# Audio tower on one core: sine slots of 32 parts with the cosine indices in place, x in eight single places, a plan that counts overlap, and early exponentials held together

## The chip, the cores and the metric

One core of a Trainium2 chip runs the whole program in one launch. The metric is device time in microseconds (us). The engines named below are PE (TensorE, matmuls), DVE (VectorE), ACT (ScalarE), POOL (GpSimd) and SP (SyncE, which here issues every DMA). Each engine works through its own list of instructions in a fixed order, and waits for another engine only through semaphores.

## The reference

Thirty-two sequences of 160,000 samples are cut into S = 313 frames of 512. A cosine transform gives h. One attention layer and one "lookup" feed-forward layer are added to it:

```python
h = einsum('bfh,kh->bfk', frames, D)
h = h + attn(layernorm(h))     # 8 heads of 64, rotary with scale,
                               # softmax * decay matrix, norm per head, silu gate
# feed-forward: 256 units n, 512 features d
theta = layernorm(h)[..., None, :] / (1 + abs(W)) + B
idx   = mod(round(theta * 4096 / 2pi), 4096)
out   = (cos_t[idx] * attn_cos).sum(-1) @ proj_cos.T \
      + (sin_t[idx] * attn_sin).sum(-1) @ proj_sin.T
h = h + silu(out)
```

The feed-forward part dominates. For each of 32 x 313 positions it needs one sine and one cosine for each of 256 x 512 pairs of unit and feature: 32,768 "parts" of 313 positions on 128 partitions (32 sequences x 256 units x 4 feature chunks), each with two transcendental values per element.

## The kernel before

**Parts, slots and rounds.** A part is one unit n, one chunk c of 128 features and one sequence: 128 x 313 elements. The 256 units are cut into 8 blocks of 32 (`UNITS`); a sequence passes through all 8, one a round, and sequences join in a staggered way given by `STARTS`. In round rd the "ring" holds the r sequences that are under way; there are 42 rounds, and r climbs from 1 to 8, stays there for 22 rounds, and falls to 1 again. Within a round, parts are taken chunk by chunk, unit by unit and sequence by sequence, and packed into *slots* of `SLOT` = 24 parts (16 at r = 1).

**What a slot does** (function `ffn_round`):

- DVE computes the table index as int16 from x and the unit's factor and offset, one instruction for each run of neighbouring sequences of one unit (line 800, `index`). A run that a slot's end cuts becomes two instructions. DVE then adds a quarter turn into a second int16 tile (`quarter`, line 816) and reduces both tiles to 12 bits with one AND/XOR (`mask`, line 823). So a slot takes two of the `N_IX` = 5 index tiles.
- ACT takes the sine of the one tile and then of the other (`sines`, line 837): two instructions of 24 x 313 = 7512 elements a slot, each into two of the `N_TRIG` = 5 half-slot f32 tiles.
- PE sums over features with 32-column weights "hot" (line 860), accumulating over the round in PSUM; at the round's end the sums are copied (line 882) and stored in DRAM.

**x.** A chunk of all the ring's sequences is loaded from DRAM by one DMA into one of `N_X` = 2 buffers of 8 places (line 785), so the next chunk's load stands in the other buffer.

**Attention.** Sequence 0 has a hand-written opening (`opening`). Each further sequence goes through `attention`, spread over the rounds by due times. It uses one set of buffers and four PSUM banks. For each pair of heads the scores' row maximum is taken and subtracted (lines 448 and 452, both DVE, into `prob`), and later `exps` takes the exponential of all eight heads in two plan operations of four heads each: one ACT instruction each (line 469) with sums by DVE (line 484), or, where the ring is narrow, twelve small ones each with the sum accumulated (line 473). The second of the two has key -1e9, so it goes first among what is ready on ACT; after it a tiny Silu activation (line 477) brings the table that holds Silu and Sin back.

**What sets the order.** The order on every engine is written out ahead of the run by a list scheduler, class `Plan`. Each operation has a key (its due place), an engine, a duration in ns, and what it reads and writes. `emit` simulates the engines: on each it takes, among what is ready by its own clock, the operation with the smallest key. An operation that waits for one on another engine becomes ready `WAIT` or `SLACK` ns after it, one that waits for its own engine at once. `lend` hands a DVE operation that has an ACT form (index, copies) to ACT when the plan sees ACT with nothing to do: line 806 is the index on ACT. SP's DMAs are planned likewise, and SP's queue runs them strictly in that order.

Of the kernel before, what the change touches and what calls it, by code (L numbers as in the profile page):

```python
# [36 lines left out]
SLOT = 24  # L37
HALF = SLOT // 2

STARTS = (0, 2, 4, *range(6, 35))  # L40
AFF = -985.0
SLACK, PATIENT, QUICK = 800.0, 18000, (2, 32)
FROM, TO, LEAD, NARROW = -900.0, -899.0, 8.0, 2
# [12 lines left out]
class Plan:  # L56
# [5 lines left out]
    OWN = 0.8  # L62

    def __init__(self):
        self.ops = []
        self.other = {}
        self.wait = []
        self.slack = self.WAIT

    def add(self, key, eng, dur, fn, r=(), w=(), other=None):  # L70
        if other:
            self.other[len(self.ops)] = other
        self.wait.append(self.slack)
        self.ops.append((key, eng, dur, fn, tuple(r), tuple(w)))
# [5 lines left out]
    def lend(self, t, e, at, free, ready, coming):  # L80

        if ready["ACT"] or free["ACT"] > t or (coming["ACT"] and coming["ACT"][0][0] <= t):
            return None
        while coming["DVE"] and coming["DVE"][0][0] <= t:
            _, i = heapq.heappop(coming["DVE"])
            heapq.heappush(ready["DVE"], (self.ops[i][0], i))
        held = sorted(ready["DVE"])[int(free["DVE"] <= t):]
        for o in sorted((o for o in held if o[1] in self.other),
                        key=lambda o: (self.other[o[1]][0] > self.ops[o[1]][2], o)):
            if True:  # L90
                start = max(free["ACT"], at[o[1]])
                if coming["ACT"] and coming["ACT"][0][0] < start + self.OWN * self.other[o[1]][0]:
                    continue
                ready["DVE"].remove(o)
                heapq.heapify(ready["DVE"])
                return o[1], start
        return None

    def emit(self):
# [31 lines left out]
        left = len(ops)  # L131
        while left:
            best = None
            for e in free:
                if ready[e]:
# [5 lines left out]
                if best is None or t < best[0]:  # L141
                    best = (t, e)
            t, e = best
            lent = self.lend(t, e, at, free, ready, coming)
            if lent:
                i, t = lent
                e = "ACT"
                dur, fn = self.other[i]
            else:
# [5 lines left out]
            fn()  # L155
            free[e] = t + dur
            end = t + dur + (self.LAND if e == "SP" else 0.0)
            left -= 1
            for j in after[i]:
                same = ops[j][1] == e and e != "SP"  # L160
                at[j] = max(at[j], end + (0.0 if same else self.wait[i]))
# [3 lines left out]
        return max(free.values())  # L165
# [3 lines left out]
def tile_audio_tower(ctx: ExitStack, tc: tile.TileContext, t: dict, out: bass.AP):  # L169
# [6 lines left out]
    N_X, N_IX, N_TRIG, N_HOT, N_PA = 2, 5, 5, 4, 4  # L176
# [185 lines left out]
    def attention(plan, keys, sq, x, eng, swap_m=None, early=False, quick=False):  # L362
# [13 lines left out]
        def residual(key, load):  # L376
            for i in range(NT):
# [20 lines left out]
        rows(plan, step("rows"), x, x.xnT, wv_d, (x.k("xnT"),), range(NT - 1, -1, -1),  # L398
             ("wv_d",))
        copy(plan, step("copy"), eng, NT * HOP, x.v[:N], W3.rearrange("n j (g d) -> n j g d", d=P),  # L400
             x.banks(0, 1, 2), hs)
        plan.add(step(), "POOL", 4000, lambda: nc.gpsimd.memset(x.v[0:1, : NT - 1], 0.0), (), hs)  # L402
# [4 lines left out]
        def rotary(g):  # L407
            key = step("rotary")
            y = x.sets[g % len(x.sets)]
            qk, kq = x.qk[g % 2], x.k("u", g % 2)  # L410
# [6 lines left out]
            else:  # L417
                copy(plan, key, eng, 2 * S, x.raw, y.W[:, 0:2, :S], y.banks(0, 1), probs[-1:])
                for i in range(2):
# [10 lines left out]
                     probs[-2:], (kq,))  # L430
# [27 lines left out]
        for half in range(2):  # L458
            for g in (2 * half, 2 * half + 1):
                rotary(g)  # L460
            for g in (2 * half, 2 * half + 1):
                scores(g)


        key = step("exps")
        for a0 in (0, H // 2):
            def exps(a0=a0):
                if eng == "DVE":
                    nc.scalar.activation(x.prob[:N, a0 : a0 + H // 2], x.prob[:N, a0 : a0 + H // 2],  # L469
                                         AF.Exp)  # L470
                for a in range(a0, a0 + H // 2):
                    for i in range(NT if eng == "ACT" else 0):
                        nc.scalar.activation(x.prob[:N, a, i, :], x.prob[:N, a, i, :], AF.Exp,
                                             accum_out=x.sm[:N, i, a : a + 1])
                if a0:

                    nc.scalar.activation(x.lu[:1, 0:1], x.lu[:1, 0:1], AF.Silu)  # L477
            plan.add(-1e9 if a0 else key, "ACT", 1400 + (7700 if eng == "ACT" else 3350), exps,
                     probs[a0 : a0 + H // 2] if early else probs if not a0 else (),
                     [*probs[a0 : a0 + H // 2], x.k("sm", a0), x.k("lu")])  # L480
        if eng == "DVE":
# [264 lines left out]
    def ffn_round(plan, k0, blk, ring, final):  # L746
# [8 lines left out]
        full = SLOT if r > 1 else 4 * N_HOT  # L755
        sizes = [full, 8, 4, 4] if not k0 else [4, 4, 8, *[full] * 7] if final else [full]
        slots, room = [[]], sizes[-1]
        for c in range(NC4):
            for n in range(UNITS):
                b0 = 0  # L760
                while b0 < r:
                    if not room:
                        slots.append([])
                        sizes = sizes[: max(1, len(sizes) - 1)]
                        room = sizes[-1]
                    nb = min(room, r - b0)
                    slots[-1].append((n, c, b0, nb, sizes[-1] - room))
                    b0 += nb
                    room -= nb
        banks, hot, xs, fs = {}, {}, {}, {}  # L770
        key = k0
        for parts in slots:
            first, last = parts is slots[0], parts is slots[-1]
            L = sum(o[3] for o in parts)
            E = L * S
            for c in dict.fromkeys(o[1] for o in parts):
                if c not in xs:
                    y, fz = xs[c], fs[c] = place("xT", N_X), place("f", N_X)
                    plan.add(key - 10, "SP", DMA_NS,
                             lambda c=c, fz=fz: nc.sync.dma_start(  # L780
                                 new("f", fz, [P, 2, UNITS], bufs=N_X), f_d[blk, :, :, c, :]),
                             ("f_d",), (("f", fz),))
                    if k0 or c > 1:
                        plan.add(key - 10, "SP", DMA_NS,
                                 lambda c=c, y=y: nc.sync.dma_start(
                                     xT[:, y, : r * S], xT_d[:, c, sq0 * S : (sq0 + r) * S]),
                                 [("xT_d", sq) for sq in ring], (("xT", y),))
            for n, c in dict.fromkeys((o[0] // 4 * 4, o[1]) for o in parts):
                if (n, c) not in hot:
                    z = hot[n, c] = place("hot", N_HOT)  # L790
                    plan.add(key - 4, "SP", DMA_NS,
# [4 lines left out]
            x = [place("ix", N_IX) for _ in range(2)]  # L796
            for n, c, b0, nb, at in parts:
                def index(x=x, n=n, b0=b0, nb=nb, at=at, y=xs[c], fz=fs[c]):
# [3 lines left out]
                        xT[:, y, b0 * S : (b0 + nb) * S],  # L802
                        f[:, 0, n : n + 1], f[:, 1, n : n + 1], ALU.mult, ALU.add)
                def index_act(x=x, n=n, b0=b0, nb=nb, at=at, y=xs[c], fz=fs[c]):
# [3 lines left out]
                        xT[:, y, b0 * S : (b0 + nb) * S], AF.Identity,  # L808
                        bias=f[:, 1, n : n + 1], scale=f[:, 0, n : n + 1])
                plan.add(key, "DVE", 276 + 0.521 * nb * S, index,  # L810
                         (("f", fs[c]), ("xT", xs[c])), (("ix", x[0], at),),
# [6 lines left out]
            plan.add(key, "DVE", 170 + 0.26 * E, quarter, every(x[0]), every(x[1]))  # L818

            def mask(x=x, E=E):  # L820

                for i in ([slice(x[0], x[1] + 1)] if x[0] < x[1] else [slice(i, i + 1) for i in x]):
                    nc.vector.tensor_scalar(ix[:, i, :E], ix[:, i, :E], LUT - 1, LUT // 2,  # L823
                                            ALU.bitwise_and, ALU.bitwise_xor)
            plan.add(key, "DVE", 170 + 0.26 * 2 * E, mask, (), [*every(x[0]), *every(x[1])])
            for k in (1, 0):
# [11 lines left out]
                plan.add(key, "ACT", 115 + 0.8333 * E, sines, every(x[1 - k]),  # L838
# [6 lines left out]

                for h, z in enumerate(w):
# [24 lines left out]
                if not last:  # L871
                    continue
                for bk, p in enumerate(banks[k]):
# [14 lines left out]
                    def store(k=k, q=q, sq=sq):  # L888
# [6 lines left out]
                        for g in range(4):  # L895
# [5 lines left out]
                             [("sums_d", sq + b, blk) for b in range(q)])  # L901

# [57 lines left out]
    xT = pools["work"].tile([P, N_X, RING * S], F32, name="xT")  # L960

    def opening(plan):

        spaces = [[trig.rearrange("p i e -> p (i e)"), 0, 4 * HALF * S],
                  [trig[:, 4], NC4 * S, HALF * S],
                  [ix.rearrange("p i e -> p (i e)").bitcast(F32), 0, N_IX * SLOT * S // 2],
                  [xT[:, 1], S, RING * S],
                  [xT[:, 0], S, RING * S]]
# [57 lines left out]
        spare = trig[:, 4, : NC4 * S].rearrange("p (c s) -> p c s", s=S)  # L1026
        xts = [xT[:, 0, :S], xT[:, 1, :S], spare[:, 2], spare[:, 3]]
        k_xts = [("xT", 0), ("xT", 1), ("trig", 4), ("trig", 4)]
# [251 lines left out]
        stands = [*(("pa", z) for z in range(N_PA)), *(("trig", z) for z in range(N_TRIG) if z != 4),  # L1280
# [25 lines left out]
    for rd in range(n_rounds):  # L1306
        events.append((key_of[rd], 3, lambda rd=rd: ffn_round(
        plan, key_of[rd], rd % life, rings[rd], rd == n_rounds - 1)))
# [15 lines left out]
    for i in range(len(times) - 1):  # L1324
        k, e = times[i] + shift[i], times[i + 1]
        narrow = len(rings[int(np.searchsorted(key_of, k, "right")) - 1]) <= NARROW
        events.append((k, 1, lambda k=k, e=e, i=i, narrow=narrow: attention(
            plan, lambda x: k + (e - k) * x, 2 + i, A, "ACT" if narrow else "DVE",
            quick=QUICK[0] <= i + 2 < QUICK[1])))
    for _, _, go in sorted(events, key=lambda y: y[:2]):  # L1330
        go()
    with tc.manual_schedule():
# [123 lines left out]
```

## Time and profile before

| what | value |
|---|---|
| time, median of 3 runs | 18152.65 us (18149.81 to 18154.47) |
| time of the profiled execution | 18155.45 us |
| its span, first to last instruction | 18153.7 us |
| instructions | 322,090 |
| mean granted TensorE clock | 0.935 |
| DMA | 943.16 MB, mean 52 GB/s |
| sines: ACT line 837 | 2780 instructions |
| index on DVE, line 800 / on ACT, line 806 | 5329 / 206 instructions |
| wait of SP's queue for PE before "hot" loads, line 792 | 7425.7 us in 1216 waits |

The span is 1.75 us shorter than that execution's time. A busy time is the union of an engine's instructions; two neighbours on ACT or DVE can overlap, so the sum of durations is larger than the busy time. What an engine did not fill of the span is idle time, and how that lies over the stages is read from the busy times in windows.

### The profile page before, as it was taken

The page shows a single profiled execution, that of the slowest core. Times are in us where ns is not written, and L with a number is a line of the kernel's source. Part 1 is how long each engine was busy: PE and PEld are TensorE (multiplying, and loading weights), DVE is VectorE, ACT ScalarE, POOL GpSimd, SP SyncE. Part 2 cuts the span into 40 slices and gives each one's busy share as a digit, 9 for nine tenths or more (in the row PEclk, how much of TensorE's full clock was granted, in tenths as well). Part 3 has the DMA queues.
Part 4 walks back from the last instruction along what each step waited for, and adds up shares of the span by engine and source line. Part 5 has one row for each costly group of instructions (what it writes and reads, how often), then busy time and mean ns, then how long its engine had stood idle before and what let it go on. Part 6 is the DMA issues. An engine that isn't in the chain of part 4 may idle for free.

```text
span 18153.7 us, 322090 instructions
## 1 busy us (share of the span) xinstructions
PE 14314.5 (79%) x146495; PEld 6447.3 (36%) x146495; DVE 17132.7 (94%) x12295; ACT 17989.7 (99%) x3448; POOL 126.5 (1%) x40
## 2 busy tenths in 40 slices
PE   8888888887778777878777787777777777766667
PEld 4434433433333333333333333333333333322222
DVE  8999999999999999999999999999999999888888
ACT  7999999999999999999999999999999999999999
POOL 0000000000000000000000000000000000000000
PEclk9999999999999999999999999999999999989889
DMA  3222211111111111111111111111111111100011
GB/s 115 74 63 64 67 56 57 53 51 47 45 52 53 53 52 41 53 54 51 51 50 47 53 53 53 52 41 53 54 51 50 48 48 54 46 28 27 28 33 58
DMA packets 603597, 943.16 MB, mean 52 GB/s; under 512 B 121290, under 2 KB 344138, under 8 KB 589430
## 3 DMA queue, kind: packets, MB, share of 16 engines
q1 hardware_dynamic: 602230, 922.56, 16.4%
q8 instruction: 1148, 18.81, 0.4%
q14 instruction: 219, 1.79, 0.0%
HBM read 818.35 MB, written 103.94 MB: 51 GB/s over the span
## 4 chain that ended last, share of the span: by engine, by line
ACT 40%; PE 18%; DVE 8%; issue 7%; DMA 0%; ACTq 0%; SPq 0%; DVEq 0%
ACT trig L837 40%; PE PS L860 15%; DVE ix L800 3%; DVE ix L823 2%; PE PS L341 2%; DVE ix L816 1%; PE PS L357 1%; ACT a_prob L469 0%; DMA a_u<-in_frames 0%; DVE part L882 0%; PE PS L561 0%; ACT L477 0%; DVE a_h L267 0%; PE PS L523 0%; ACTq L837 0%
## 5 line engine op out<-in xcount | busy, mean ns | idle before, releaser
L837 ACT ACTIVATE trig<-ix 128x7512 f32<-128x7512 int16 (+2 forms) x2780 | 17384.1, 6346 | 50.1 <-PE PS L860 30.6
L860 PE MATMUL PS<-trig,hot 128*32 128x313 f32 x131072 | 10449.9, 463 | 3662.4 <-ACT trig L837 3594.1
L860 PEld LDWEIGHTS PS<-trig,hot 128*32 128x32 f32 x131072 | 4391.7, 117 | 9590.2 <-ACT trig L837 4876.7
L800 DVE TENSOR_SCALAR ix<-xT,f 128x2504 int16<-128x2504 f32 (+7 forms) x5329 | 6418.7, 1264 | 90.4 <-ACT trig L837 67.1
L823 DVE TENSOR_SCALAR ix<-ix 128x7512 int16<-128x7512 int16 (+3 forms) x1668 | 5583.9, 3362 | 42.5
L816 DVE TENSOR_SCALAR ix<-ix 128x7512 int16<-128x7512 int16 (+2 forms) x1390 | 2908.8, 2093 | 553.3 <-ACT trig L837 450.7
L357 PE MATMUL PS<-a_xnT,a_ring 128*128 128x313 f32 x4960 | 1468.1, 439 | 8.9 <-DVE a_prob L425 6.9
L341 PE MATMUL PS<-a_ring,a_u 128*105 128x512 f32 x2232 | 1067.4, 611 | 53.6 <-DMA a_u<-in_frames 19.6
L357 PEld LDWEIGHTS PS<-a_xnT,a_ring 128*128 128x128 f32 x4960 | 893.4, 189 | 588.4 <-issue 276.5
L341 PEld LDWEIGHTS PS<-a_ring,a_u 128*105 128x105 f32 x2232 | 349.9, 171 | 629.3 <-issue 585.3
L341 PE MATMUL PS<-a_ring,a_xnT 128*105 128x512 f32 x744 | 353.9, 608 | 3.5 <-DVE a_xnT L267 1.8
L500 PE MATMUL PS<-ident,a_prob 105*105 105x105 f32 x2232 | 288.8, 272 | 70.5 <-DVE a_prob L512 47.1
L448 DVE TENSOR_REDUCE a_mx<-PS 105x2 f32<-105x626 f32 x372 | 298.6, 803 | 29.0 <-PE PS L443 28.9
L512 DVE TENSOR_TENSOR a_prob<-PS,a_u 105x939 f32<-105x939 f32 x248 | 280.3, 1130 | 38.4 <-PE PS L500 34.3
L500 PEld LDWEIGHTS PS<-ident,a_prob 105*105 105x105 f32 x2232 | 236.5, 176 | 223.7 <-issue 140.6
L452 DVE TENSOR_TENSOR a_prob<-PS,a_mx 105x626 f32<-105x626 f32 x372 | 301.3, 810 | 12.8
L443 PE MATMUL PS<-a_u 64*105 64x313 f32 x1488 | 258.9, 453 | 8.5 <-DVE a_prob L452 7.0
L523 PE MATMUL PS<-a_prob,a_h 105*64 105x313 f32 x1488 | 240.9, 443 | 6.6 <-DVE a_prob L512 6.5
L484 DVE TENSOR_REDUCE a_sm<-a_prob 105x6 f32<-105x1878 f32 x112 | 228.8, 2103 | 8.6 <-ACT a_prob L469 8.6
L402 POOL MEMSET a_h<- 1x1024 f32 x31 | 124.0, 4002 | 15023.3 <-DVE a_h L267 14393.9
L806 ACT ACTIVATE ix<-xT,f 128x313 int16<-128x313 f32 (+6 forms) x206 | 195.3, 1008 | 0.2
L425 DVE TENSOR_TENSOR a_prob<-PS,a_prob 128x1252 f32<-128x1252 f32 x124 | 180.7, 1457 | 10.5 <-PE PS L357 9.8
(157 smaller groups left out, 2606.0 us busy)
## 6 DMA issues: line engine op xcount, KB each, us to landing
hot<-in_hot SPq DMA_DIRECT2D x1344, 128.0 KB
xT<-xT_d SPq DMA_DIRECT2D x88, 1252.0 KB
a_u<-in_decay SPq DMA_DIRECT2D x248, 260.5 KB
a_ring<-in_proj SPq DMA_DIRECT2D x128, 256.0 KB
a_ring<-in_dct SPq DMA_DIRECT2D x124, 256.0 KB
a_ring<-wv_d SPq DMA_DIRECT2D x124, 256.0 KB
a_ring<-in_wq SPq DMA_DIRECT2D x124, 256.0 KB
a_ring<-in_wk SPq DMA_DIRECT2D x124, 256.0 KB
```

The source lines that it names most:

```text
L341: lambda c=c, i=i, k=k, to=to: nc.tensor.matmul(x.W[:N, to, :], lhsT[:, c, ROW0[i] : ROW0[i] + N], x.ring[k], start=(c == 0), stop=(c == N ...
L357: lambda c=c: nc.tensor.matmul(y.W[:, bank, :S], w[:, c, :], x.xnT[:, c, :], start=(c == 0), stop=(c == NC4 - 1)),
L443: nc.tensor.matmul(y.W[:N, b + a, :S], qk[a * DH : a * DH + DH, 0, ROW0[i] : ROW0[i] + N], qk[a * DH : a * DH + DH, 1, :], start=True, sto ...
L448: lambda b=b, m=m, y=y: nc.vector.tensor_reduce(m[:N], y.W[:N, b : b + 2, :S], AX.X, ALU.max),
L452: lambda i=i, b=b, m=m, y=y: nc.vector.tensor_tensor(x.prob[:N, 2 * g : 2 * g + 2, i, :], y.W[:N, b : b + 2, :S], m[:N].unsqueeze(2).to_br ...
L500: nc.tensor.transpose(y.W[:N, jj, ROW0[i] : ROW0[i] + N], x.prob[:N, a, i, ROW0[j] : ROW0[j] + N], ident[:N, :N],)
L512: nc.vector.tensor_tensor(x.prob[:N, a], y.W[:N, :NT, :S], w3, ALU.mult)
L800: nc.vector.tensor_scalar(ix[:, x[0], at * S : (at + nb) * S], xT[:, y, b0 * S : (b0 + nb) * S], f[:, 0, n : n + 1], f[:, 1, n : n + 1], A ...
L816: nc.vector.tensor_scalar(ix[:, x[1], :E], ix[:, x[0], :E], float(LUT // 4), None, ALU.add)
L823: nc.vector.tensor_scalar(ix[:, i, :E], ix[:, i, :E], LUT - 1, LUT // 2, ALU.bitwise_and, ALU.bitwise_xor)
L837: nc.scalar.activation(o, i, AF.Sin, bias=-PI32, scale=ANG)
L860: nc.tensor.matmul(sums_W[:, p, :][g * 32 : g * 32 + 32, :S], now["hot", hot[n // 4 * 4, c]][:, n % 4, k, :], trig[:, z, at * S : (at + 1) ...
```

## The change

- **Slots.** `SLOT` is 32 where r > 3, 24 where r is 2 or 3, 16 where r = 1.
- **Index tiles.** Where r > `PAIR` = 3 a slot has one index tile (`alone`): mask, sines from it, then the quarter turn is added *in the same tile*, masked again (AND only), and the second sines read it. The second half of a slot is put into the plan later (`late`, `LAG` = 2 keys after the slot), so other slots' sines go between. `N_IX` and `N_TRIG` are 4.
- **x.** Instead of two buffers there are 8 single places (`PLACES`), filled from the left for even chunks and from the right for odd ones (`home`); a chunk's load is cut into pieces of at most 4 places (`PIECE`) and each piece waits for the last index instruction of the old chunk on those places. The index instructions of a chunk's first and last unit are cut at the same places.
- **Plan.** Durations now overlap: an engine is free again `OVER` (85 ns DVE, 100 ns ACT) before an operation's end, and an operation that depends on one of its own engine becomes ready `AFTER` = 35 ns after that one's end.
- **Early exponentials.** For sequences 1 to 6 (`burst`) the scores of all heads are computed together when all rotary parts are done, each with its own maximum, and ACT takes the exponential straight from PSUM with the maximum as bias and the sum accumulated. From the first to the last of these 24 the plan holds ACT and DVE to this group (`held`; DVE may also take operations up to 900 ns).
- **Stagger.** `STARTS` is new: 48 rounds; r is 7 in 19 of them, 8 in 4.

The diff, cut:

```diff
-SLOT = 24
-STARTS = (0, 2, 4, *range(6, 35))
+SLOT, HALF = 32, 16
+PLACES, PIECE, LAG, AHEAD, PAIR = 8, 4, 2.0, 0.5, 3
+N_F, N_IX, N_TRIG, N_HOT, N_PA = 2, 4, 4, 4, 4
+STARTS = (0, 3, 5, 8, 10, 10, 12, 13, 15, 16, 17, 18, 19, 20, 21, 23, 25, *range(25, 31), *range(32, 41))
...
+    OVER = {"DVE": 85.0, "ACT": 100.0}
+    AFTER = 35.0
...
+    def next_held(self, e, at, free, ready, coming):
+        some = [(max(free[e], at[i]), self.ops[i][0], i) for _, i in (*ready[e], *coming[e])
+                if self.group.get(i) == self.held or (e == "DVE" and self.ops[i][2] <= self.SHORT)]
...
             free[e] = t + dur
+            free[e] -= min(self.OVER.get(e, 0.0), dur / 2)
             end = t + dur + (self.LAND if e == "SP" else 0.0)
...
-                at[j] = max(at[j], end + (0.0 if same else self.wait[i]))
+                at[j] = max(at[j], end + (self.AFTER if same else self.wait[i]))
...
+        def together():
...
+                    nc.scalar.activation(x.prob[:N, hd, i, :], x.W[:N, b, :S], AF.Exp, bias=m, scale=1.0,
+                                         accum_out=x.sm[:N, i, hd : hd + 1])
...
+                plan.add(-1e9 + z, "DVE", 490, lambda b=b, m=m: nc.vector.tensor_reduce(
+                    m, x.W[:N, b, :S], AX.X, ALU.max, negate=True), x.banks(b), (km,), group=gid)
...
-        full = SLOT if r > 1 else 4 * N_HOT
+        full = SLOT if r > 3 else 24 if r > 1 else 4 * N_HOT
...
+        def home(c, r):
+            return PLACES - r if c % 2 else 0
...
-                        plan.add(key - 10, "SP", DMA_NS,
-                                 lambda c=c, y=y: nc.sync.dma_start(
-                                     xT[:, y, : r * S], xT_d[:, c, sq0 * S : (sq0 + r) * S]),
-                                 [("xT_d", sq) for sq in ring], (("xT", y),))
+                    for y, some in before[c] if k0 or c > 1 else ():
+                        q = sq0 + y - home(c, r)
+                        plan.add(key - 10, "SP", XD * some,
+                                 lambda c=c, y=y, q=q, some=some: nc.sync.dma_start(
+                                     xT[:, y : y + some, :].rearrange("p b s -> p (b s)"),
+                                     xT_d[:, c, q * S : (q + some) * S]),
...
+            one = 170 + 0.26 * E
+            if alone:
+                plan.add(key, "DVE", one, mask, every(x[0]), every(x[0]))
+                half_slot(1, key)
+                plan.add(key + AHEAD, "DVE", one, quarter, every(x[0]), every(x[0]))
+                plan.add(key + AHEAD, "DVE", one, lambda m=mask: m(half=0), every(x[0]), every(x[0]))
+                late.append((key + L / SLOT + LAG, half_slot))
```

The code of the two exponential operations that sequences from 7 on use is the old one, unchanged.

## The prediction

> **What bounds the kernel now.** First the page's busy times, then the same by windows.
>
> ```profile
> PE 14314.5 (79%) x146495; PEld 6447.3 (36%) x146495; DVE 17132.7 (94%) x12295; ACT 17989.7 (99%) x3448; POOL 126.5 (1%) x40
> ...
> 0.00:500.00 500.00, 437.51 (x3085) 220.87 (x3089) 438.51 (x732) 393.95 (x344) 6.58 (x10) 0.94 0.36 110
> 500.00:1000.00 500.00, 443.08 (x3985) 207.55 (x3976) 474.59 (x530) 489.02 (x156) 2.05 (x1) 0.95 0.25 74
> 2500.00:3000.00 500.00, 406.82 (x4079) 184.03 (x4069) 487.66 (x371) 497.77 (x89) 2.79 (x1) 0.94 0.20 60
> 6000.00:6500.00 500.00, 394.85 (x4080) 175.43 (x4080) 478.73 (x313) 499.94 (x86) 5.25 (x1) 0.94 0.17 53
> 16000.00:16500.00 500.00, 343.00 (x3784) 142.20 (x3784) 430.60 (x241) 500.00 (x81) 0.00 (x0) 0.90 0.08 26
> ```
>
> In a window's line the busy times after the width are PE, PEld, DVE, ACT, POOL. ACT is busy 17989.7 of 18153.7 us, so only 164 us are idle: 106 in the first 500 us (the opening), 29 from 500 to 3500, 9 from 3500 to 15500, 20 after. So ACT's list sets the time. Close behind is DVE, at 478.7 of 500 in the middle, 430.6 once attention is over (from about 15500). The window 2500 to 3000 shows what a DVE at 487.7 does: ACT loses 2.2 us. The chain of waits agrees only roughly (ACT 40%), because it also follows PE and DVE when they are nearly as late.
>
> Then ACT's and DVE's groups, each shape by itself: count, busy, mean ns.
>
> ```profile
> L837 ACT ACTIVATE trig<-ix 128x7512 f32<-128x7512 int16 x2658 | 16916.5, 6457 | 42.5 <-PE PS L860 26.3 <-issue 6.0 <-DVE ix L823 4.5
> L837 ACT ACTIVATE trig<-ix 128x5008 f32<-128x5008 int16 x100 | 432.5, 4370 | 5.3 <-PE PS L860 3.3 <-DVE ix L823 0.8 <-ACT a_h L265 0.6
> L469 ACT ACTIVATE a_prob<-a_prob 105x3756 f32<-105x3756 f32 x56 | 183.7, 3327 | 0.3
> L477 ACT ACT_TABLE_LOAD x31 | 39.8, 1283 | 0.5
> L1175 ACT ACTIVATE ix<-PS,trig 105x313 f32<-105x313 f32 x24 | 12.2, 520 | 15.0 <-DVE trig L1170 15.0
> ...
> L823 DVE TENSOR_SCALAR ix<-ix 128x15024 int16<-128x15024 int16 x1064 | 4333.9, 4073 | 32.4
> L800 DVE TENSOR_SCALAR ix<-xT,f 128x2504 int16<-128x2504 f32 x2811 | 4293.5, 1579 | 56.8 <-ACT trig L837 46.8
> L816 DVE TENSOR_SCALAR ix<-ix 128x7512 int16<-128x7512 int16 x1329 | 2827.9, 2128 | 468.0 <-ACT trig L837 370.4 <-ACT ix L806 4.9 <-DVE ix L800 2.3
> L800 DVE TENSOR_SCALAR ix<-xT,f 128x313 int16<-128x313 f32 x358 | 136.2, 444 | 5.4 <-ACT trig L837 4.0
> L823 DVE TENSOR_SCALAR ix<-ix 128x10016 int16<-128x10016 int16 x41 | 113.5, 2769 | 1.3
> ```
>
> **The change on ACT, part by part.** Counts of the changed program are from its built instruction lists.
>
> *Fewer sines.* The two shapes give (6457 - 4370) / 2504 = 0.8335 ns an element. A 7512 sine occupies 16916.5 / 2658 = 6364 ns, of which 6261 are elements, so an instruction costs 103 ns beyond them. The elements stay; 2780 sines become 2154 (1824 of them 128x10016): 626 x 0.103 = -65 us.
>
> *Index lent to ACT.* Line 806 took 195 us for 206 instructions. The new plan lends 129, nearly all of one to three sequences. By shape from the old rows (313 at 0.57, 626 at 0.86, 939 at 1.12, 1565 and 2191 at 1.7 and 2.2) this is 98: -97 us. The work goes to DVE.
>
> *Table loads.* The new list holds the sequence "load, exponential of four heads, load, one sine, load, exponential of four heads, load, Silu" 25 times, where the old one has the two exponentials side by side. The second exponential depends on the first; it now becomes ready 35 ns after the first's end, while ACT is free 100 ns before that end, so the plan puts a sine between. Loads go from 66 to 114: 48 x 1.283 = +62 us, on the engine that bounds.
>
> What a load costs beyond its own row is seen in the timeline:
>
> ```profile
> 207.55 8.65 ACT L837 ACTIVATE trig<-ix 128x5008 f32<-128x5008 int16 x2
> 216.22 1.28 ACT L473 ACT_TABLE_LOAD   x1
> 217.51 0.47 ACT L473 ACTIVATE a_prob<-a_prob 105x313 f32<-105x313 f32 x1
> ```
>
> The sines end at 216.20, the load at 217.50, the next starts at 217.51: nothing but the row. The Trainium skill ("ScalarE: Activation LUTs", What ACT_TABLE_LOAD costs) counts a drain of 1380 ns on top, 2.66 us a switch, and advises doing all of one set before switching, which speaks against this order; by it the 48 loads would be +128 us and the forecast 66 us later. The row decides.
>
> *Exponentials.* 56 large ones (183.7) become 50, 164. 72 small ones of sequences 1 to 3 (rows of line 473, 32.3 + 13.7 with the accumulator read) become 144 from PSUM, for which line 1175 gives (12.2 + 4.8) / 24 = 0.708 each: 102. Together 230 to 266: +36 us. Copies lent to ACT change by -4.
>
> ACT's sum is -65 - 97 + 62 + 36 - 4 = -68, so it is busy about 17922 us.
>
> **What the change does to DVE.** Index instructions go from 5329 to 7055, since a unit has mostly 7 sequences and slots end inside it. From 444 at 313 elements and 1579 at 2504 the fixed part is 282 ns, less some 50 of overlap (window 5000 to 7000: durations sum to 1969.5, busy 1908.3, 1235 instructions): 1726 x 0.23 = +400, and +45 for 272 parts no longer lent. Masks: per part (2128 + 4073) / 24 = 258 against 3 x 2769 / 32 = 260, no difference, down to -100 if the third pass overlaps too. The early group saves 72 subtractions of 0.81, 72 double maxima of 0.80 and 12 sums of 2.04 and adds 144 single maxima of about 0.48 (half of the double's elements): about -70. Sum +275 to +375, all in the shade of ACT as long as DVE keeps up.
>
> Does it? At r = 8 a slot of 24 cost DVE 3 x 1579 + 2128 + 4073 - 5 x 50 = 10.69 us, 445 ns a part. At r = 7 a slot of 32 has 32/7 + 6/7 = 5.4 index instructions: 5.43 x 282 + 10016 x 0.518 + 3 x 2769 - 8.4 x 50 = 14.6 us, 456 a part, +2.4%. In a middle window some 413 of 478.7 us are of this kind (the rest, about 65, is attention), so DVE comes to 488.6 of 500: the state of window 2500 to 3000. From 3000 to 15500 there are 25 such windows. ACT idle there lies between 0.06 (window 6000) and 2.2 (window 2500) each, 2 to 55 us; slots now last 16.9 us of ACT with four in hand, where 2.5 slots of 12.7 were. I take 27, 18 more than before.
>
> **Waits.** *Early groups*: while ACT is held it idles when a maximum is late. Line 1175 is the same chain: 15.0 us of idle in 24. Six groups make 0 to 90; I take 7, as in the opening the rotary parts stood between and here all scores are ready first. DVE's relief before 1800 should save about as much of the 29. *x in single places*: 250 loads of two or four places can no longer run ahead. In the built order the DVE work between the last read of four old places and the first of the new ones is 9.4 us in the median and under 5 us in 7 of 131 cases. The first two loads of the opening (412 KB) are used 3.7 us after issue; 626 KB at the 363 GB/s of that stage is some 4.3. So it is hidden, if SP issues on time; the queue gains 498 DMAs at about 0.4 us. If all that cover went, each change of chunk would stop DVE for 4.3. *Half-slots*: PE must empty two before the next but one sine; 32 parts x 10449.9 / 65536 = 5.1 us of 8.45, a margin of 3.3 where the old rotation left 6.36 - 3.83 = 2.5 at worst. I take nothing for it.
>
> **Sum.** Idle: opening 106, then 29, middle 27, tail 20, in all 182, less some 4 for a lighter start. 17922 + 178 = 18100 span, 18102 with the 1.75 outside. The profiled execution stood 2.8 above the median: 18100 us, 0.29% less.
>
> **Rivals.**
>
> *Better (18057).* The early stage loses 25 of its 29 and the middle stays at 9: 18100 - 25 - 18 = 18057. For it: DVE drives less there. Against it: the held groups.
>
> *Saved and lost again (18150).* The middle idles the full 55 and the groups 30: 18100 + 28 + 23 = 18151. For it: static order, and DVE at 98%. Against it: deeper slots.
>
> *Slower (18236): x lands late and DVE becomes the bound.* The place is the 33 rounds of the middle, 4 changes of chunk each, 132. DVE's spare there is 25 x (500 - 488) = 300 us, so it decides from 2.3 us a change. Midway to the full 4.3, at 3.3, the excess is 132 x 3.3 - 300 = 136: 18236. For it: SP waits 7425.7 us for PE before hot loads, and x stands in that queue. Against it: the 9.4 us of cover.
>
> **How the numbers follow.** Forecast 0.45 (18070 to 18130), better 0.18, lost again 0.21, slower 0.16. A measurement tells 0.2%, 36 us, from no change: faster is below 18116, slower above 18189. The forecast gives 0.38 of its 0.45 to faster and 0.07 to no change; with the others: faster 0.56, same 0.27 (0.20 of "lost again"), slower 0.17. The range 18030 to 18200 leaves out the lower end of "better" and most of "slower".
>
> **What would show it.** Sines: 2154 at a mean near 8.54 us for 10016 elements, 8.45 busy. ACT busy near 17922; loads 114, of them 25 before a lone sine. DVE near 488 in the middle windows; ACT there at 498 or more. ACT's waits on early maxima under 10 us. Wrong, if ACT's idle in the middle passes 60, or index instructions of DVE wait for x loads.

## The result: slower, 18233.94 us

| | median, us | ratio to the kernel before (95%) |
|---|---|---|
| before | 18152.65 (18149.81 to 18154.47) | |
| changed | 18233.94 (18225.33 to 18237.58) | 1.0044 [1.003, 1.0059] |

The forecast was 18100. The profiled execution took 18236.04, its span is 18234.3. First the page's busy times, then the windows of the changed kernel (the prediction shows the same views of the kernel before).

```profile
PE 15505.7 (85%) x146495; PEld 6834.4 (37%) x146495; DVE 17242.4 (95%) x14037; ACT 17943.5 (98%) x2927; POOL 119.9 (1%) x40
...
0.00:500.00 500.00, 432.61 (x2832) 212.03 (x2833) 408.97 (x777) 353.60 (x326) 2.75 (x9) 0.92 0.37 110
500.00:1000.00 500.00, 448.71 (x4012) 198.78 (x4013) 474.45 (x547) 480.78 (x143) 7.17 (x2) 0.96 0.26 73
2500.00:3000.00 500.00, 432.44 (x4157) 201.15 (x4157) 487.06 (x419) 498.98 (x71) 17.16 (x2) 0.96 0.19 55
6000.00:6500.00 500.00, 445.15 (x4123) 198.41 (x4117) 483.69 (x373) 498.78 (x67) 3.44 (x1) 0.96 0.18 54
16000.00:16500.00 500.00, 350.29 (x3819) 146.50 (x3808) 428.07 (x246) 498.54 (x61) 0.00 (x0) 0.86 0.09 26
```

ACT did get less to do: 17943.5 against 17989.7, 46 us less. But it idles 290.8 us in place of 164.0. The surprise is in the second column: PE is busy 15505.7 us, 1191 more, with the same 146,495 matmuls; in the window from 6000 it went from 394.85 to 445.15. A lower granted clock is not the reason: its mean was 0.946, and 0.935 before. The groups of ACT and PE:

```profile
L949 ACT ACTIVATE trig<-ix 128x10016 f32<-128x10016 int16 x1824 | 15422.1, 8545 | 47.7 <-PE PS L973 24.6 <-issue 12.6 <-ACT trig L949 5.8
L949 ACT ACTIVATE trig<-ix 128x7512 f32<-128x7512 int16 x252 | 1611.1, 6458 | 55.0 <-PE PS L973 48.7 <-DVE ix L935 3.3 <-issue 1.2
L547 ACT ACT_TABLE_LOAD x50 | 64.2, 1283 | 0.9
L949 ACT ACT_TABLE_LOAD x25 | 32.1, 1283 | 0.4
...
L973 PE MATMUL PS<-trig,hot 128*32 128x313 f32 x131072 | 11511.4, 456 | 2527.5 <-ACT trig L949 2513.6
```

The last number group of a line is the engine's idle time before it and who ended it. Sines wait for PE (92.5 us in all, 30.6 before): PE is late in emptying the half-slots (a half-slot is one of the buffers that the sines are written to).

ACT's idle by stage, us, is the window's length less ACT's busy time:

| | ACT busy | 0-500 | 500-2000 | 2000-3500 | 3500-15500 | after |
|---|---|---|---|---|---|---|
| before | 17989.7 | 106.1 | 21.3 | 7.5 | 8.8 | 20.4 |
| changed | 17943.5 | 146.4 | 60.0 | 7.2 | 51.8 | 25.4 |

### The profile page after: what moved, and what is told of

Read it like the earlier page. It is cut to its first block, busy times and chain, and to the rows that moved or that the text cites. A ratio compares the mean times of both kernels' runs of the same rounds, so it can differ in the third digit from the quotient of the medians.

```text
span 18234.3 us, 322492 instructions
## 1 busy us (share of the span) xinstructions
PE 15505.7 (85%) x146495; PEld 6834.4 (37%) x146495; DVE 17242.4 (95%) x14037; ACT 17943.5 (98%) x2927; POOL 119.9 (1%) x40
## 5 line engine op out<-in xcount | busy, mean ns | idle before, releaser
L949 ACT ACTIVATE trig<-ix 128x10016 f32<-128x10016 int16 (+3 forms) x2154 | 17336.7, 8134 | 134.7 <-PE PS L973 92.5
L973 PE MATMUL PS<-trig,hot 128*32 128x313 f32 x131072 | 11511.4, 456 | 2527.5 <-ACT trig L949 2513.6
L973 PEld LDWEIGHTS PS<-trig,hot 128*32 128x32 f32 x131072 | 4814.8, 115 | 8965.3 <-ACT trig L949 3254.9
L912 DVE TENSOR_SCALAR ix<-xT,f 128x2191 int16<-128x2191 f32 (+7 forms) x7055 | 6854.5, 1030 | 543.3 <-ACT trig L949 535.2
L935 DVE TENSOR_SCALAR ix<-ix 128x10016 int16<-128x10016 int16 (+2 forms) x1989 | 5649.4, 2845 | 26.5 <-DVE ix L912 0.5
L929 DVE TENSOR_SCALAR ix<-ix 128x10016 int16<-128x10016 int16 (+3 forms) x1077 | 2839.0, 2636 | 110.3 <-ACT trig L949 97.1
L394 PE MATMUL PS<-a_xnT,a_ring 128*128 128x313 f32 x4960 | 1563.9, 448 | 23.3 <-DVE a_prob L471 11.4
L590 DVE TENSOR_TENSOR a_prob<-PS,a_u 105x939 f32<-105x939 f32 x248 | 280.6, 1131 | 50.3 <-PE PS L578 50.1
L601 PE MATMUL PS<-a_prob,a_h 105*64 105x313 f32 x1488 | 295.1, 455 | 13.6 <-DVE a_prob L590 13.6
L494 DVE TENSOR_REDUCE a_mx<-PS 105x2 f32<-105x626 f32 x300 | 235.4, 806 | 8.9 <-PE PS L489 8.6
L498 DVE TENSOR_TENSOR a_prob<-PS,a_mx 105x626 f32<-105x626 f32 x300 | 240.7, 807 | 0.0
L378 PEld LDWEIGHTS PS<-a_ring,a_xnT 128*105 128x105 f32 x744 | 111.9, 170 | 199.4 <-issue 172.8
```

What stands on the lines that cost most here:

```text
L378: lambda c=c, i=i, k=k, to=to: nc.tensor.matmul(x.W[:N, to, :], lhsT[:, c, ROW0[i] : ROW0[i] + N], x.ring[k], start=(c == 0), stop=(c == N ...
L394: lambda c=c: nc.tensor.matmul(y.W[:, bank, :S], w[:, c, :], x.xnT[:, c, :], start=(c == 0), stop=(c == NC4 - 1)),
L494: lambda b=b, m=m, y=y: nc.vector.tensor_reduce(m[:N], y.W[:N, b : b + 2, :S], AX.X, ALU.max),
L498: lambda i=i, b=b, m=m, y=y: nc.vector.tensor_tensor(x.prob[:N, 2 * g : 2 * g + 2, i, :], y.W[:N, b : b + 2, :S], m[:N].unsqueeze(2).to_br ...
L590: nc.vector.tensor_tensor(x.prob[:N, a], y.W[:N, :NT, :S], w3, ALU.mult)
L601: nc.tensor.matmul(y3.W[b * DH : (b + 1) * DH, 3, :S], x.v[:N, jj, g, b * DH : (b + 1) * DH], x.prob[:N, 2 * g + b, jj, :], start=(jj == 0 ...
```

## The experiments

Times are medians; "before" on the same chips was 18149.6 to 18155.1. Edits are against the changed kernel unless a base is named.

**e1, the old stagger.**

```diff
-STARTS = (0, 3, 5, 8, 10, 10, 12, 13, ..., *range(32, 41))
+STARTS = (0, 2, 4, *range(6, 35))
```

> The changed kernel with the old STARTS (42 rounds, 8 sequences in 22 of them) and nothing else. Theory PE: with 7 sequences the two PSUM banks hold 4 and 3, so PE needs as many steps as for 8; of its 1061 us of added busy time on the sums line, the old stagger takes back at least 650, PE falls to about 14450 to 14800 us, ACT's idle in the middle (3500 to 15500) falls from 52 to under 25 us, and index instructions on DVE fall from 7055 to 5684; time about 18150 to 18180. Rival, place by place loads of x: with 8 sequences every place is shared by neighbouring chunks, so no load can run ahead; then DVE waits for x, ACT's idle in the middle rises over 52 and the time stays above 18234. Rival, overlap counted too tightly in the plan: idle stays as it is, time 18190 to 18230 (only the index instructions matter little, as DVE is not the bound).

Measured 18184.91, ratio 1.0019 [1.0008, 1.003]: 49 us back, 5 short of what was expected. The windows from 500 and of the middle:

```profile
500.00:2000.00 1500.00, 1329.96 (x11962) 610.09 (x11963) 1402.93 (x1408) 1452.93 (x435) 23.34 (x5) 0.96 0.22 67
3500.00:15500.00 12000.00, 9792.18 (x98937) 4240.00 (x98941) 11391.92 (x7666) 11993.03 (x1582) 74.98 (x22) 0.93 0.16 51
```

PE in the middle is 9792 in place of 10492 us and ACT's idle there 7.0 in place of 51.8. What ACT's sines wait for PE in the middle, in the changed kernel and then in e1 (us in total, times, longest):

```profile
ACT trig L949 <- PE PS L973: 23.0, 27, 2.9
ACT trig L949 <- PE PS L973: 2.2, 4, 0.9
```

PE's total fell by 764 of its 1191; the other 427 came without the new stagger, and no run traces them. The rival with x is out for the middle: with 8 sequences no place is free early, and DVE waits there 3.1 us for x. Outside the middle the old stagger does bring such waits, 33.0 us in all of DVE and ACT in e1, against 4.8 in the changed kernel.

The mechanism can be read inside the changed kernel's own trace. Two stretches of rounds with 7 and with 8 sequences follow each other (DVE's index there is mostly 128x2191, seven sequences, from 10250, and 128x2504, eight, from 10750). The windows of PE's sums line alone:

```profile
10250.00:10550.00 300.00, 194.30 (x2188) 81.80 (x2180) 0.97 0.17 49
10750.00:11050.00 300.00, 170.62 (x2176) 68.41 (x2168) 0.93 0.17 49
```

The same number of matmuls takes 88.8 ns each with 7 and 78.4 with 8, 13% more. The slower stretch has the higher granted clock (0.97). Each PSUM bank takes the 32-column sums of four sequences side by side; seven make a bank of four and a bank of three. If the bank of three took a whole step as the bank of four does, 8/7 would be 14%.

That is not the whole of it. The same line in rounds of 3 and of 6 in the changed kernel, then in rounds of 6 in e12 (below), which has the same stagger and half-slots of 12 parts in place of 16:

```profile
900.00:1200.00 300.00, 201.31 (x2100) 79.47 (x2097) 0.98 0.23 66
3600.00:3900.00 300.00, 185.07 (x2128) 78.06 (x2132) 0.92 0.19 56
```

```profile
3600.00:3900.00 300.00, 163.28 (x2138) 68.69 (x2140) 0.94 0.18 55
```

With 3 sequences, a bank of three alone, a matmul takes 95.9 ns, 22% above the 78.4 and not a full third (at a granted clock of 0.98 against 0.93). With 6 the program fills a bank of four and, with two units side by side, the other bank as well; yet a matmul takes 87.0 ns with half-slots of 16 parts, which cut a unit's six sequences, and 76.4 with half-slots of 12, which do not. So the larger half-slots cost PE steps too; no run parts the two at 7.

**e2, both exponentials in one plan operation.**

```diff
-            for a0 in (0, H // 2):
-                def exps(a0=a0):
+            def exps_all():
+                for a0 in (0, H // 2):
...
-            plan.add(-1e9 if a0 else key, "ACT", 1400 + (7700 if eng == "ACT" else 3350), exps,
+            plan.add(key, "ACT", 2600 + 2 * (7700 if eng == "ACT" else 3350), exps_all, probs,
```

> The changed kernel with the two exponential operations of sequences 7 to 31 made one plan operation, so that no sine comes between. Theory of the table loads: 50 loads fewer (114 to 64) x 1.283 = 64 us off ACT's busy time (17943 to about 17879), and as ACT is the bound, the time falls by 55 to 65, to about 18170 to 18180. Rival, the loads lie in time that ACT would idle anyway: time above 18215.

Measured 18180.23, ratio 1.0016 [1.0005, 1.0027]: 54 us back. ACT's timeline in the changed kernel, then the same place in e2:

```profile
9322.84 1.28 ACT L547 ACT_TABLE_LOAD   x1
9324.13 3.34 ACT L547 ACTIVATE a_prob<-a_prob 105x3756 f32<-105x3756 f32 x1
9327.49 1.28 ACT L949 ACT_TABLE_LOAD   x1
9328.79 8.55 ACT L949 ACTIVATE trig<-ix 128x10016 f32<-128x10016 int16 x1
9337.36 1.28 ACT L547 ACT_TABLE_LOAD   x1
9338.65 3.34 ACT L547 ACTIVATE a_prob<-a_prob 105x3756 f32<-105x3756 f32 x1
9342.01 1.28 ACT L555 ACT_TABLE_LOAD   x1
```

```profile
9294.39 1.28 ACT L547 ACT_TABLE_LOAD   x1
9295.68 6.56 ACT L547 ACTIVATE a_prob<-a_prob 105x3756 f32<-105x3756 f32 x2
9302.26 1.28 ACT L553 ACT_TABLE_LOAD   x1
```

Four loads become two, and each costs its 1.283 us and little more: the next instruction starts within 0.02 us. ACT's busy time fell by 66.9, 1.34 for each of 50 loads; 14 of it came back as idle in the middle (65.6), where PE sets the pace.

**e3, no held groups.**

```diff
-FROM, TO, LEAD, NARROW, BURSTS = -900.0, -925.0, 4.0, 1, 7
+FROM, TO, LEAD, NARROW, BURSTS = -900.0, -925.0, 4.0, 1, 0
-    attention(plan, lambda x: FROM + (TO - FROM) * x, 1, A, "ACT", None, True)
+    attention(plan, lambda x: FROM + (TO - FROM) * x, 1, A, "ACT", None, True, burst=False)
```

> The changed kernel with the held early groups taken out (sequences 1 to 6 by the old order of scores and exponentials). Theory that the held groups cost: ACT's idle before 2000 us falls from 206 to about 150, and 36 us of small exponentials go; time about 18170. Rival, the stagger sets the early stage: DVE gets back 72 subtractions and 12 sums, idle before 2000 stays near 200 or rises, time 18230 to 18290.

Measured 18241.5, ratio 1.0051: 8 us worse. The first 500 us gain 24 (idle 122.2), but 500 to 2000 lose 8 and ACT gets 27 more. So the groups cost the changed kernel nothing.

**e4, the plan without overlap.**

```diff
-    OVER = {"DVE": 85.0, "ACT": 100.0}
-    AFTER = 35.0
+    OVER = {"DVE": 0.0, "ACT": 0.0}
+    AFTER = 0.0
```

> The changed kernel with the plan's overlap set to nothing (OVER 0, AFTER 0), as the old plan counted. The second exponential is then ready when ACT is free, so the 50 added loads go too (64 us), but 323 index instructions are lent to ACT instead of 129 (about +150 us on ACT). Theory that the tight plan makes ACT wait: idle falls from 291 by at least 60 and the time is near 18230 or less in spite of the lending. Rival, the lending decides: ACT busy rises to about 18030, time 18280 to 18330.

Measured 18297.63, ratio 1.008. Both halves of the expectation came: idle fell by 79 to 212, but ACT's busy time rose by 140 to 18083 through the lending, although 50 loads went. Over the whole run the overlap clock is a net gain of 64.

**e5, e1 and e2 together.**

> The changed kernel with the old STARTS and the exponentials in one operation. If the two causes lie in different places, their gains add: 18185 - 54 = about 18130, ACT busy near 17880, idle near 235, and it beats the kernel before. Rival, the loads only filled time in which ACT would wait for PE: time above 18160.

Measured 18124.41, ratio 0.9983 [0.9973, 0.9993], faster than the kernel before. The gains add: 49 + 54 = 103, measured 110.

**e6, which engine the stagger loads.** Base e5.

```diff
-... else [(home(c, r), r)]:
+... else [(home(c, r) + z, 4) for z in (0, 4)] if r == 8 and n % 2 else [(home(c, r), r)]:
```

> As e5_both, but in the rounds of 8 sequences every second unit's index instruction is cut into two of 4, so that DVE has 7000 index instructions, as many as the changed kernel (7055), and PE's work stays that of the old stagger. Theory PE: the middle's idle stays under 25 us and the time within 15 us of e5_both, though DVE gets some 300 us more. Rival DVE: the added index instructions are what starves ACT; middle idle 45 or more, time 35 to 60 us above e5_both.

Measured 18135.92: 12 us more, where single executions of either kernel lie up to 21 apart. DVE rose by 217 us, to 97.0% of the middle (the changed kernel: 96.3%), and ACT's idle there is 13.6. So 1320 added index instructions, nearly as many as the new stagger added (1371), cost some 12 of the 49. The rest is put down to PE by elimination, with the rates and waits above; no run changes PE's steps alone.

**e7, eight side by side after the new first starts.** Base e5.

```diff
-STARTS = (0, 2, 4, *range(6, 35))
+STARTS = (0, 3, 5, 8, *range(9, 37))
```

> As e5_both, but STARTS is (0, 3, 5, 8, 9, 10, ... 36): the changed kernel's first four starts, then one a round, so that 8 sequences stand side by side in the middle. Theory: the changed kernel was only 14 us behind before at 3500 us, e1 39; so this takes some 20 us off e5_both, about 18105 to 18115. Rival: the later starts just shift the early idle, time within 10 us of e5_both or above.

Measured 18155.97, ratio 1.0 [0.9991, 1.0009], 32 above e5: a miss. ACT idles 26.9 from 2000 to 3500 in place of 11.2, and 13 us more are busy.

**e8, slots of 24.** Base e5.

```diff
-        full = SLOT if r > 3 else 24 if r > 1 else 4 * N_HOT
+        full = SLOT if r in (4, 5) else 24 if r > 1 else 4 * N_HOT
```

> As e5_both, but slots of 24 parts in place of 32 wherever there are more than 5 sequences (2714 sines in place of 2122). Theory that slots of 32 bring what an instruction costs ACT beyond its elements, 0.103 us: 592 x 0.103 = 61 us more ACT, time 50 to 65 us above e5_both. Rival, smaller slots let PE and DVE follow more closely and win it back: within 20 us of e5_both.

Measured 18299.89, 175 above e5. ACT has 70 more to do (61 expected), and idles 110 more, 78 of that in the middle. So with one index tile a slot and four half-slots, the larger slot is worth more than the sum gave it. ACT's waits there are spread (36 us for PE, 26 with no releaser seen, 19 for its own sine before), and which of them is the cause was not tried.

**e9 to e11, the early stage.** Base e5. e9 leaves sequence 1 without the held group (the second edit of e3). e10 cuts the same trig memory into five half-slots of 12 parts where r is at most 3:

```diff
-                w = sorted(place("trig", N_TRIG) for _ in range(2))
+                few = r <= PAIR
+                cap = 12 if few else HALF
+                w = sorted(place("trig5" if few else "trig", 5 if few else N_TRIG) for _ in range(2))
+                view = flat[:, : 60 * S].rearrange("p (i e) -> p i e", i=5) if few else trig
```

> As e5_both, but sequence 1 does not use the held group (sequences 2 to 6 still do). Theory: the opening's extra idle, 141 against 106 us in the first 500, is the held group of sequence 1 and the scores put together before it; idle there falls to 110 to 120 and the time by 10 to 30, to about 18095 to 18115. Rival: as in e3 the gain is given back by 1000 us, time within 8 us of 18124.

> As e5_both, but in rounds of 1 to 3 sequences the same trig memory is cut into five half-slots of 12 parts, as in the kernel before, in place of four of 16. Theory: ACT's waits for PE before sines (some 70 us in the changed kernel before 2000 us, most of them before 7512 and 5008 sines) come from having only four half-slots there; they fall to about 30 and the time by 20 to 40, to about 18085 to 18105. Rival: PE itself is behind there (three of four column groups used), waits stay, time within 8 us of 18124.

> Both edits on top of e5_both: if both theories hold, about 18070 to 18090.

e9: 18159.37, 35 worse than e5, a miss: the first 500 us idle 175.8, as one sine waits 23.4 us for its index. e10: 18104.02, ratio 0.9975 [0.9965, 0.9984], 20 better, the low end of what was expected. e11: 18127.82, a miss like e9: 24 of e9's loss come back on top of e10. ACT's waits before 2000 us in e5, then in e10 (us in total, times, longest):

```profile
ACT trig L946 <- PE PS L970: 51.1, 37, 6.5
```

```profile
ACT trig L952 <- PE PS L976: 19.5, 18, 3.2
```

The fifth half-slot takes away 32 us of waits for PE.

**e12, the new stagger in the kernel before.** The same STARTS line, the other way.

> The kernel before with the new STARTS and nothing else. Theory PE: its PE time grows by some 700 to 1000 us and ACT is made to wait in the middle; as its plan also lends 313 index instructions to ACT in place of 206 (some 100 us), time 18240 to 18320. Rival: the old slots with five half-slots take the stagger without loss, and only the lending shows: 18200 to 18240; if the stagger is harmless, under 18180.

Measured 18317.02, ratio 1.0092 [1.0072, 1.0112]: alone it costs the old kernel 166 us. ACT is 123 us busier, 114 of it lent index (195 to 309), and idles 41 more, 31 of that in the middle; sines wait 50.1 us for PE before.

**f1, f3, f4, what is left of the early loss.** Base e10. f1 has no held groups (both edits of e3). f3 lets the plan count overlap only after 2000 us of its clock, f4 does both:

```diff
-            free[e] -= min(self.OVER.get(e, 0.0), dur / 2)
+            free[e] -= min(self.OVER.get(e, 0.0), dur / 2) if t > self.FIRM else 0.0
-                at[j] = max(at[j], end + (self.AFTER if same else self.wait[i]))
+                at[j] = max(at[j], end + ((self.AFTER if t > self.FIRM else 0.0) if same else self.wait[i]))
```

> As e10_five_halves, without any held group (sequences 1 to 6 by the old order of scores). Theory groups: ACT has done more by 500 us (about 500 parts in place of 460) and the idle of the first 500 falls from 139 to about 115; time 18075 to 18100. Rival clock: the groups save DVE work where it is short, so without them ACT is further behind at 2000 us; time 18110 to 18140.

> As e10_five_halves, but the plan counts without overlap (and without the 35 ns) up to 2000 us of its own time, with it after. Theory clock: ACT's idle before 2000 falls from 177 to about 140, while 26 more index instructions are lent (about 20 us), so the time falls by 10 to 20, to 18085 to 18095. Rival groups: idle before 2000 stays above 165 and the time at 18100 or above.

> Both edits on top of e10_five_halves: the early stage is then ordered as in the kernel before; if the early loss (23 us by 3500 against the kernel before) is of these two alone, it goes, 18075 to 18085. If more is left, it is the place by place loads of x or the old stagger's tighter due times.

None came as its theory had it. f1: 18207.83, 104 worse. f3: 18103.99, equal to e10 (ratio 0.9974 [0.9964, 0.9983]). f4: 18128.85, 25 worse than f3. So on this base the held groups are worth 25 to 104 us, where e3 found 8 on the changed kernel; and the clock makes some of the idle of the first 500 us (139.2 to 119.3 in f3), but that gain is spent on lent work: by 2000 us both have begun the sines of 3008 parts. Idle in the opening is no loss in itself. e10 is then still 23 us behind the kernel before at 3500 us (5696 parts against 5740). Up to half of that may be x: before 3500 us an index lent to ACT waits 11.2 us for a load of x in e10, and the kernel before shows no wait for x. This was not tried; the cause stays open.

## Why the prediction was wrong, point by point

**ACT's sum: right in its terms, 21 us too low.** Expected 17922, measured 17943.5. A sine of 10016 takes 8455 ns of busy time (8450 expected), there are 2154 and 114 loads. Of the 21 us between, 18 are sines: some 7 in those of 10016 (4 ns each) and 7 in those of 7512, which now occupy 1611.1 / 252 = 6393 ns where 6364 was reckoned. The table loads cost their row, as e2 shows. The drain of 1380 ns that the Trainium skill ("ScalarE: Activation LUTs", What ACT_TABLE_LOAD costs) adds to each did not appear: a load came to 1.34 us.

**The step that failed: "half-slots", PE, priced at nothing.** It took 5.1 us of PE for 32 parts from the old mean, most of which are rounds of eight, while the same prediction counted DVE's index for seven. At seven 32 parts need 64 x 88.8 = 5.7 us. That alone would still leave 2.8 of the 3.3 us of margin; what the margin left out is attention, whose matmuls share PE. PE is busy 87.4% of the middle in place of 79.1%. In the 17 us before each of the 27 sines that wait for PE there, attention's matmuls fill 31 to 64% of PE's time, before all sines of the middle 25% on average (worked out from the changed kernel's trace). The new stagger is worth 49 us by e1, some 12 of which are DVE's by e6.

**Idle: 178 expected, 290.8 measured.** Of the 113, the middle has 25 (51.8 for 27), the first 500 us 44, 500 to 3500 38, the tail 5. In the middle the range given (2 to 55) held by luck: it was reckoned from DVE's share, and what ACT is seen to wait for there is mostly PE (29 us; 11 have no releaser, 2 are DVE's). For early sines the prediction had no term for five half-slots becoming four: 62.4 us of waits for PE before 2000, where there were 14.6, and 20 us of time by e10. For the held groups it took 7 us; ACT waits 19.1 for their maxima, past the 10 that it named as a sign. In e10, with the old stagger and the fifth half-slot, ACT still idles 191 us before 3500 where 131 were forecast; what makes these 60 is open.

**DVE keeps up: right, its sum too high.** Middle 96.3% of the window (97.7 expected), and its waits are mostly for ACT (535.2 us before the index line). Its busy time rose by 110 us where 275 to 375 were added up. The durations did rise by 453, but neighbours now overlap by 980 us in all in place of 636: an index instruction behind another starts 87 ns before that one's end, where 50 were taken.

**x: hidden, as the sum had it, with the new stagger.** DVE waited 4.8 us for x loads in all (in e1 33.0 with ACT's, as said above):

```profile
L912 DVE TENSOR_SCALAR ix<-xT,f 128x1252 int16<-128x1252 f32 x775 | 701.8, 931 | 110.3 <-ACT trig L949 106.6 <-DMA xT<-xT_d 3.5
L912 DVE TENSOR_SCALAR ix<-xT,f 128x626 int16<-128x626 f32 x853 | 488.8, 604 | 80.9 <-ACT trig L949 79.2 <-DMA xT<-xT_d 1.3
```

**The rivals.** The slower rival's number (18236) was met, its mechanism was not: x is not late and DVE is not the bound. "Saved and lost again" named the right kind of loss and the wrong engine.

**What part of the change did what.** Stagger +49, split exponentials +54, all else together -22 (what is left of the measured +81) to -31 (e5 against the kernel before on the same chip). The prediction had counted the table loads (+62), so of the two it is the stagger that it missed.

## What to carry to other kernels

A shape that changes the work of the bounding engine's neighbour must be priced on every engine: seven in place of eight was counted for DVE and forgotten for PE, where side-by-side matmuls that do not fill a step cost nearly a whole one. After a change to a planner's clock, compare the built order for pairs that must stay neighbours; 35 ns of care there bought two table loads a sequence. Idle time at the start tells little; count finished work at a fixed time instead.

## What was not expected of the hardware

Matmuls of 32 columns side by side: three cost nearly the time of four, 88.8 against 78.4 ns a matmul at 7 and 8 sequences and 95.9 at 3, with the median duration of a single one at 427 ns in the windows of 7 and of 8. A buffer's edge that cuts a set has a like price, 87.0 against 76.4 at 6. So the durations show nothing of it, only busy time per matmul does.
